# PSUM tiles per bank, reordered normalization, smaller one-hot chunks, ordered gathers and transposes with a strided output in a convolution, attention and expert kernel

## The chip, the cores and the metric

The kernel runs on one core of a Trainium2 chip. The metric is the device time of one execution in microseconds (us), taken as the median over several runs. One execution is also recorded by the hardware profiler; its span is the time from the first to the last recorded event, and its own device time lies a little above the span.

A core has several engines with queues of their own: TensorE (PE) multiplies matrices and transposes, VectorE (DVE) and ScalarE (ACT) do elementwise work, reductions and copies, GpSimd (POOL) does small vector work and issues indirect DMAs (gathers and scatters by a list of row numbers), SyncE (SP) issues most plain DMAs. SBUF is the on-chip memory of 128 partitions; PSUM is the memory that TensorE writes its results to, in banks of 512 float32 values per partition.

## The reference

The input `x` is one image of 256 channels and 48 x 48 = 2304 positions (tokens). Three layers follow one another:

1. A convolutional attention: `q`, `k` and `v` are 1x1 projections of the normalized image. They are split into 4 heads by a reshape, which makes one sequence of 9216 rows of 64 values, and `O = softmax(q k^T) v` runs over all 9216 rows. An output projection and a residual follow.
2. A "slice" attention: each token has softmax weights `sw` over 64 slices. Keys, queries and values are averaged over the tokens with these weights (`qs`, `ks`, `vs`), an attention runs among the 64 slices of each of 8 heads, and its result is spread back to the tokens with the same weights: `out = (tok spread by sw) Wout + bout`, with a residual.
3. A mixture of experts: every token is layer-normalized, a linear gate picks the best 2 of 8 experts by its logits, and each chosen expert computes `gelu(x W1 + b1) W2 + b2`. The two results, weighted by a softmax over the two logits, are added to the token.

The result goes out with channels first, as it came. Cut to its core:

```python
x = x + conv_attn(group_norm(x))      # qf, kf, vf: (9216, 64); softmax(qf kf^T / 8) vf; Wo, bo
t = tokens(x)                         # (2304, 256)
h = layer_norm(t) @ W0 + b0           # slice attention
sw = softmax(h @ Ws + bs)             # (2304, 64)
qs, ks, vs = (sum_n(sw * part) / sum_n(sw) for part in qkv(h))
tok = softmax(qs ks^T / sqrt(32)) vs  # per head, 64 x 64
t = t + (sw spread tok) @ Wout + bout
u = layer_norm(t)                     # experts
top_w, top_i = top_k(u @ Wg + bg, 2); top_w = softmax(top_w)
for e in range(8):
    t += w_dense[:, e] * (gelu(u @ W1[e] + b1[e]) @ W2[e] + b2[e])
return channels_first(t)
```

## The kernel before, in words

`layers` (L63 on) computes everything up to a token-major array `t_d` in DRAM (2304 rows of 256 values), and `to_columns` (L1238) brings it back to channels-first. The class `InOrder` (L49 to 59) wraps an engine so that its instructions keep the order in which they are written; `pe`, `dve`, `act` and `pool` are such wrappers (L78), and therefore most instructions have L57 in the profile, whatever line asked for them. What is called through `nc.` directly is placed by the scheduler of the tile framework by its own estimates. The indirect DMAs go through `pool` too, but the record of the execution shows that GpSimd did not issue the gathers in the order written.

*Start.* `x` is loaded by SP in four pieces (two for each half of the channels, 1152 positions each, L153 to 156). VectorE computes statistics over pieces of 384 positions as they come (L258 to 261), TensorE prepares the projection weights meanwhile.

*Attention.* 18 query blocks by 36 pairs of key blocks, from about 36 us to 1240 us. It is untouched.

*Slice attention* (L728 to 880). Sums over the tokens are in two banks, `bank_den` and `bank_pts`. A tile `psc` of two banks takes the scores of the 64 slices (L804); their maximum `am`, the difference `a` and an exponential follow (L815 to 821), then the values and transposes on TensorE.

*y0 stage* (L881 to 922). The 18 token tiles of 128 tokens are worked in groups of 6, 6, 4 and 2. For each tile TensorE spreads the slice result back, `swT` by `tw` (256 channels and 8 gate logits, so 264 columns), and adds the residual. The output of tile after tile goes into seven banks in turn: den, pts, the two halves of `psc`, and three more, `py0` to `py2`. VectorE takes the statistics of a tile (`bn_stats`, `bn_aggr`), ScalarE copies it to `t_sb`; for two tiles VectorE adds instead. At the end of a group VectorE adds a small constant to the variances (`ve`), GpSimd raises them to the power −1/2 (`rstd_t`) and forms `shift`, and SP stores the group to `t_d`. `normed` (L869) applies the normalization to a group on ScalarE, one instruction for each tile, into `tn2` (two buffers, so the third group waits until the first is stored) and stores it to `tn_d` in DRAM. Group 0 is normed after group 1's tiles, the others after the stage.

*Routing* (L933 to 1078). VectorE forms the logits `lg` for all tokens from the statistics, finds the best and second-best expert (`first_max`), and marks both in `both`. TensorE sums these marks over the tokens (`pto`, `pin`), and VectorE derives from the sums the position of each token and choice in a list of slots of 128 rows; 43 slots are planned, 36 of them certain to be used (`SURE`). The list itself is made by TensorE: for each of 36 (choice, token tile) pairs, a matrix `in_row` (which row of a slot, on VectorE, laid over the storage of `t_sb`) is multiplied with `what` (which slot, and the weight; the first half from VectorE and the second, in `find_tile`, from ScalarE, one instruction for each pair) and all are summed in `pw`. `find_tile` forms `in_tile` for 9, 9 and 18 pairs; the loop at L1051 works through the pairs in chunks of 3, 6, 9, 9, 6 and 3. From `pw` come the row numbers `slot_t` and the weights `slot_w`. `busy(n, spin)` issues n matmuls on TensorE whose result nobody reads.

*Experts* (L1086 to 1217). For each slot GpSimd gathers 128 normalized rows from `tn_d` by `slot_t` (`rows`), TensorE transposes them (`turn`), the two layers follow, and GpSimd adds the result `y` to `t_d` by an indirect DMA with addition. SP loads the first layer's weights of the slot's expert, 1 MB each. Rows for the slots that may be unused go into tiles of their own, `late_xs` (7 of them), and are written in the loop to come one per slot from slot 17 on.

*Back to channels first* (L1238 to 1262). Five blocks of 512 tokens (the last 256) are loaded with consecutive tokens in one partition. For each block and half of the channels, TensorE transposes four tiles into a bank `pt`, one after the other, and VectorE (first half) or ScalarE (second half) copies the bank to `ob`, writing with a stride so that the tokens come into their order. SP stores `ob`; there are three buffers of it.

Of the kernel before, what the change touches and what calls it, by code (L numbers as in the profile page):

```python
# [27 lines left out]
S = 64  # L28
# [34 lines left out]
def layers(  # L63
# [88 lines left out]
    x_sb = l0.tile([P, 2, NT], FP, name="x_sb")  # L152
    for c in range(2):  # L153
        for h in range(2):
            cols = slice(h * NT // 2, (h + 1) * NT // 2)
            nc.sync.dma_start(out=x_sb[:, c, cols], in_=x_v[:, c, cols])

# [571 lines left out]
    gating = ExitStack()  # L729
    gp = gating.enter_context(tc.tile_pool(name="gate", bufs=1))  # L730


    with tc.tile_pool(name="sa", bufs=1) as sa, sums_done, tc.tile_pool(
        name="ps_sc", bufs=1, space=PSUM
    ) as ps_sc:
        tw = sa.tile([P, C + E], FP, name="tw")
        psc = ps_sc.tile([P, 2, 512], FP, name="psc")
        banks = [bank_den, bank_pts, psc[:, 0, :], psc[:, 1, :]]

# [4 lines left out]
        with tc.tile_pool(name="ps_b", bufs=3, space=PSUM) as ps_b:  # L744
# [54 lines left out]
            for u in range(2):  # L799
                for r in range(4):  # L800
                    v, w = divmod(r, 2)
                    rows = slice(r * D1, (r + 1) * D1)
                    pe.matmul(
                        psc[w * S : (w + 1) * S, v, u * S : (u + 1) * S],  # L804
                        qk[rows, u, 0, :], qk[rows, u, 1, :], start=True, stop=True,
                    )
# [7 lines left out]

            by_head = [P, 2, 2, S]  # L815
            sc = psc[:, :, 0 : 2 * S].rearrange("p v (u t) -> p v u t", u=2)
            am = sa.tile([P, 2, 2], FP, name="am")
            dve.tensor_reduce(am, sc, AX.X, ALU.max)
            a = sa.tile(by_head, FP, name="a")
            dve.tensor_tensor(a, sc, am.unsqueeze(3).to_broadcast(by_head), ALU.subtract)  # L820
            act.activation(a, a, AF.Exp, scale=float(D1) ** -0.5)
            act.copy(vs, pv)
# [58 lines left out]
        shift = const.tile([P, NTT], FP, name="shift")  # L881
        with tc.tile_pool(name="ps_y0", bufs=1, space=PSUM) as ps_y0, tc.tile_pool(
            name="norm", bufs=2
        ) as norm:
            banks = cycle(banks + [ps_y0.tile([P, 512], FP, name=f"py{k}") for k in range(3)])
            groups = [(0, 6), (6, 6), (12, 4), (16, 2)]
            by_dve = (4, 6)
            for g, (i0, n) in enumerate(groups):
# [31 lines left out]
                )  # L920
                if g == 1:
                    normed(*groups[0])
            for group in groups[1:]:
                normed(*group)


# [6 lines left out]
    with gating, tc.tile_pool(name="onehot", bufs=1) as oh, tc.tile_pool(  # L933
# [43 lines left out]
        dve.tensor_sub(e2, m2, m1)  # L977
        act.activation(e2, e2, AF.Exp)
        act.activation(gp.tile([P, 1], FP, name="table"), e2[:, 0:1], AF.Gelu)
        upto = gp.tile([P, E, NTT], FP, name="upto")  # L980
# [69 lines left out]
        k = 0  # L1050
        for n in (3, 6, 9, 9, 6, 3):  # L1051
            ks = slice(k, k + n)
# [34 lines left out]
    with tc.tile_pool(name="ps_h", bufs=1, space=PSUM) as ps_h, tc.tile_pool(  # L1087
# [14 lines left out]
        late_xs = iter([fp.tile([P, C], FP, name=f"late_xs{s}") for s in range(SURE, NSL)])  # L1102

        def rows(s, xs):
            pool.indirect_dma_start(
                out=xs, out_offset=None, in_=tn_d[:, :],
                in_offset=bass.IndirectOffsetOnAxis(ap=slot_t[:, s : s + 1], axis=0),
                bounds_check=NT + P - 1, oob_is_err=True,
            )
            return xs  # L1110
# [36 lines left out]
        def second(s, hid, meanwhile):  # L1147
# [3 lines left out]
            for f in range(NHC):  # L1151
# [12 lines left out]
            dve.tensor_scalar(y, y, slot_w[:, s : s + 1], None, ALU.mult)  # L1164
            pool.indirect_dma_start(
                out=t_d[:, :], out_offset=bass.IndirectOffsetOnAxis(ap=slot_t[:, s : s + 1], axis=0),
# [25 lines left out]
        for s in range(SURE):  # L1192
# [17 lines left out]
            skip_runtime_bounds_check_because="it is a sum of counts, cut at NSL",  # L1210
        )
        with ExitStack() as more:  # L1212
            for s in range(SURE, NSL):
                more.enter_context(tc.If(used > s))
                if s + 1 < NSL:
                    w1[s + 1] = load_w1(s + 1)
                second(s, first(s, xT.pop(s), w1.pop(s)), lambda: turn_next(s + 1))
# [3 lines left out]
def kernel(ctx: ExitStack, tc: tile.TileContext, *args):  # L1221
# [16 lines left out]
    def to_columns():  # L1238

        sp = InOrder(tc, nc.sync)  # L1240
        with tc.tile_pool(name="fin", bufs=1) as fin, tc.tile_pool(name="fin3", bufs=3) as fin3, tc.tile_pool(
# [5 lines left out]
            for (t0, n), tt in zip(TBLOCKS, tts):  # L1247
                ob = fin3.tile([P, 2, 512], FP, name="ob", tag="ob")
                for c in range(2):
                    pt = ps_f.tile([P, 512], FP, name="pt", tag="pt")  # L1250
                    for k in range(n // P):
                        nc.tensor.transpose(  # L1252
                            pt[:, k * P : (k + 1) * P], tt[:, k, c * P : (c + 1) * P], ident
                        )

                    dst = ob[:, c, 0:n].rearrange("q (p k) -> q k p", p=P)
                    src = pt[:, 0:n].rearrange("q (k p) -> q k p", p=P)
                    if c == 0:
                        nc.vector.tensor_copy(dst, src)  # L1259
                    else:  # L1260
                        nc.scalar.copy(dst, src)  # L1261
                sp.dma_start(out=out_v[:, :, t0 : t0 + n], in_=ob[:, :, 0:n])

# [39 lines left out]
```

## Time and profile before

| what | us |
|---|---|
| median of three runs | 1619.2 (1617.68, 1619.2, 1619.96) |
| the profiled execution, device time | 1616.37 |
| its span | 1614.3 |
| TensorE busy in the span | 1569.7 |
| attention (36 to 1240) | 1204, TensorE busy 1201.98 |
| y0 stage (1263 to 1275.4) | 12.4 |
| routing (1275.4 to 1305.3) | 29.9 |
| experts (1305.3 to 1592) | 286.7, TensorE busy 283.79 |
| back to channels first (1592 to 1614.3) | 22.3, TensorE busy 6.62 |

In a row by stage, each engine has its busy time and in brackets its number of instructions; then comes the clock that TensorE was granted, as a share of full speed, the mean busy share of the 16 DMA engines, and what they moved in GB/s. A row of waits names who waited for what, the sum in us, how often, and the longest. A row in order of time has the start, the time taken, the engine, the line, the operation, what it writes and reads, how many instructions are drawn together, and in square brackets the idle time just before and what ended it.

### The profile page before, as it was taken

Reading aid. Unit: us, or ns where it says so; the run is one execution under the profiler, and the core shown is the slowest. Engines: PE = TensorE matmul, PEld = TensorE weight load, DVE = VectorE, ACT = ScalarE, POOL = GpSimd, SP = SyncE. Lnnn points to the kernel's source line nnn. Section 1 sums busy time; section 2 is a strip of 40 time slices with the busy share of each in tenths; the row PEclk is TensorE's granted clock in tenths of the full one; section 3 lists DMA queues with packets and bytes.
Section 4 is the critical chain, followed back from the end, with each engine's and each line's share of the span. In section 5 each row is a group of like instructions: output and inputs, shape, how many; then the busy total and the mean of one; then the engine's idle time right before and its main releaser. Section 6 shows DMA issues by size and latency. Waiting matters only on the chain. (4 is left out here: it accounts for less than half of the span.)

```text
span 1614.3 us, 31899 instructions
## 1 busy us (share of the span) xinstructions
PE 1569.7 (97%) x13231; PEld 786.4 (49%) x13231; DVE 1043.5 (65%) x1367; ACT 824.0 (51%) x1143; POOL 140.7 (9%) x128
## 2 busy tenths in 40 slices
PE   7999999999999999999999999999999799999995
PEld 3633343333333333333333333333334589999995
DVE  6577777777786877877868778788687721111112
ACT  2355555555655655556556555565554433333322
POOL 0000000000000000000000000000000143333321
PEclk9999999999999999999999999999999999999998
DMA  4000000000000000000000000000001856666655
GB/s 138 0 1 1 1 1 1 1 1 1 1 1 1 2 1 1 1 1 2 1 1 1 1 1 1 1 1 1 1 2 58 295 186 187 179 181 189 174 156 184
DMA packets 38246, 79.26 MB, mean 49 GB/s; under 512 B 3613, under 2 KB 23914, under 8 KB 37962
## 3 DMA queue, kind: packets, MB, share of 16 engines
q1 hardware_dynamic: 30410, 66.35, 12.3%
q0 software_dynamic: 7680, 10.75, 3.8%
q8 instruction: 108, 1.77, 0.5%
q14 instruction: 48, 0.39, 0.1%
HBM read 64.64 MB, written 12.45 MB: 48 GB/s over the span
## 5 line engine op out<-in xcount | busy, mean ns | idle before, releaser
L57 ACT ACTIVATE p<-s 128x1024 f32<-128x1024 f32 x648 | 663.5, 1024 | 489.5 <-PE s L57 479.4
L57 DVE TENSOR_TENSOR acc<-acc,p 128x1024 f32<-128x1024 f32 x612 | 748.0, 1222 | 251.8 <-ACT p L57 244.0
L57 PE MATMUL av<-p,v_sb 64*64 64x512 f32 x5184 | 676.0, 590 | 1.0 <-DVE up L57 0.7
L57 PE MATMUL s<-q,kk 64*64 64x512 f32 x5184 | 676.4, 590 | 0.0
L57 PEld LDWEIGHTS s<-q,kk 64*64 64x64 f32 x5184 | 202.2, 133 | 351.8 <-issue 181.1
L57 PEld LDWEIGHTS av<-p,v_sb 64*64 64x64 f32 x5184 | 196.1, 131 | 358.0 <-ACT p L57 202.6
L57 ACT ACTIVATE hid<-ph,bcol 128x128 f32<-128x128 f32 x312 | 89.4, 368 | 200.4 <-PE ph L57 199.7
L57 PE MATMUL py<-w_sb,hid 128*128 x624 | 147.1, 379 | 0.0
L57 PEld LDWEIGHTS ph<-xT,w 128*128 128x128 f32 x1248 | 145.3, 192 | 2.7 <-DVE xT L57 0.8
L57 PE MATMUL ph<-xT,w 128*128 128x128 f32 x1248 | 145.7, 275 | 0.5 <-DVE xT L57 0.5
L57 POOL TENSOR_TENSOR rstd_t<-ve,mhalf 128x1 f32<-128x1 f32 (+3 forms) x22 | 28.0, 1272 | 1233.4 <-DVE ve L57 1233.4
L57 DVE COPY xT<-pt 128x256 f32<-128x256 f32 x40 | 17.0, 424 | 171.6 <-PE pt L57 171.6
L57 PEld LDWEIGHTS py<-w_sb,hid 128*128 128x128 f32 x624 | 112.8, 190 | 12.2
L57 POOL DMA_INDIRECT t_d<-y,slot_t x39 | 61.7, 1583 | 98.3 <-DVE y L57 87.9
L57 DVE TENSOR_TENSOR y<-py,b_bc 128x256 f32<-128x256 f32 x39 | 16.6, 425 | 68.6 <-PE py L57 68.6
L57 POOL DMA_INDIRECT xs<-tn_d,slot_t x36 | 38.4, 1067 | 106.3 <-PE pt L57 82.1
L57 DVE RECIPROCAL rinv<-pb 128x256 f32<-128x256 f32 x18 | 31.5, 1749 | 0.0
L57 DVE TENSOR_TENSOR acc<-p 128x1024 f32<-128x1024 f32 x18 | 22.1, 1226 | 9.7 <-ACT p L57 9.7
L314 DVE TENSOR_SCALAR q<-pp,bcol 64x512 f32<-64x512 f32 (+1 forms) x30 | 20.8, 695 | 7.7 <-PE pp L297 7.4
L57 DVE TENSOR_REDUCE up<-av 128x512 f32<-128x1024 f32 x18 | 21.9, 1216 | 0.0
L319 ACT ACTIVATE kk<-pp,bcol 128x512 f32<-128x512 f32 (+1 forms) x10 | 6.4, 645 | 22.1 <-PE pp L301 22.1
L297 PE MATMUL pp<-t_sb,WqT 128*128 128x512 f32 (+1 forms) x40 | 17.6, 562 | 0.0
(281 smaller groups left out, 617.9 us busy)
## 6 DMA issues: line engine op xcount, KB each, us to landing
w<-in_L_ffn_W_dram SPq DMA_DIRECT2D x40, 1024.0 KB, 5.4
w_sb<-in_L_ffn_W_dram SPq DMA_DIRECT2D x8, 1024.0 KB, 13.1
x_sb<-in_x_dram SPq DMA_DIRECT2D x4, 576.0 KB
t<-t_d SPq DMA_DIRECT2D x4, 512.0 KB, 6.3
out_dram<-ob SPq DMA_DIRECT2D x4, 512.0 KB
t_d<-t_sb SPq DMA_DIRECT2D x2, 768.0 KB, 4.9
tn_d<-tn SPq DMA_DIRECT2D x2, 768.0 KB, 4.0
b_bc<-in_L_ffn_b_dram SPq DMA_DIRECT2D x1, 1024.0 KB
```

The lines of the kernel that those rows point to most:

```text
L57: return self.tc.keep_in_program_order(getattr(self.engine, name)(*args, **kwargs))
L297: nc.tensor.matmul(pq[:, 0:tn], WqT[:, c, cols], xn[:, c, toks], start=(c == 0), stop=(c == 1))
L314: nc.vector.tensor_scalar(dst, pq[rows, 0:tn], bcol[rows, B_Q + m : B_Q + m + 1], 0.125, ALU.add, ALU.mult,)
L319: nc.scalar.activation(kk[:, m, toks], pk[:, 0:tn], AF.Identity, bias=bk_m)
```

## The change

- The second half of `x` by channels is loaded in pieces of 1152, 768 and 384 positions; there are five loads in place of four.
- `psc` becomes two tiles of one bank each. The maximum, the difference and the exponential of the scores are made for each bank.
- `normed` of groups 0 and 1 comes after the whole y0 stage, followed by 13 `busy` matmuls. `normed` of groups 2 and 3 comes in the routing, after the exponential `e2` and ahead of the activation that loads the table for Gelu. The pool `norm` therefore lives longer; it still has two buffers.
- The chunks are 3, 6, 6, 3, 6, 6, 3, 3.
- Every indirect DMA is given an order behind the one written before it (`indirect`). On GpSimd the seven gathers of `late_xs` now come one in each of the slots 17 to 23; before, they came among the first gathers.
- In `to_columns` the transposes write with a stride, so that the bank holds the tokens in their order, and the copies to `ob` read and write contiguously. ScalarE's copies keep their written order, and the last two blocks are stored by ScalarE's queue in place of SP's.

```diff
-    for c in range(2):
-        for h in range(2):
-            cols = slice(h * NT // 2, (h + 1) * NT // 2)
-            nc.sync.dma_start(out=x_sb[:, c, cols], in_=x_v[:, c, cols])
+    for c, pieces in enumerate(((1152, 1152), (1152, 768, 384))):
+        at = 0
+        for n in pieces:
+            nc.sync.dma_start(out=x_sb[:, c, at : at + n], in_=x_v[:, c, at : at + n])
+            at += n
...
+    norm = gating.enter_context(tc.tile_pool(name="norm", bufs=2))
...
-        psc = ps_sc.tile([P, 2, 512], FP, name="psc")
-        banks = [bank_den, bank_pts, psc[:, 0, :], psc[:, 1, :]]
+        psc = [ps_sc.tile([P, 512], FP, name=f"psc{v}") for v in range(2)]
+        banks = [bank_den, bank_pts, *psc]
...
-            dve.tensor_reduce(am, sc, AX.X, ALU.max)
-            a = sa.tile(by_head, FP, name="a")
-            dve.tensor_tensor(a, sc, am.unsqueeze(3).to_broadcast(by_head), ALU.subtract)
-            act.activation(a, a, AF.Exp, scale=float(D1) ** -0.5)
+            a = sa.tile([P, 2, 2, S], FP, name="a")
+            for v in range(2):
+                dve.tensor_reduce(am[:, v, :], sc[v], AX.X, ALU.max)
+            for v in range(2):
+                dve.tensor_tensor(a[:, v], sc[v], bc(am[:, v, :], [P, 2, S]), ALU.subtract)
+                act.activation(a[:, v], a[:, v], AF.Exp, scale=float(D1) ** -0.5)
...
-                if g == 1:
-                    normed(*groups[0])
-            for group in groups[1:]:
+            for group in groups[:2]:
                 normed(*group)
+            busy(13, spin)
...
         act.activation(e2, e2, AF.Exp)
+        for group in groups[2:]:
+            normed(*group)
         act.activation(gp.tile([P, 1], FP, name="table"), e2[:, 0:1], AF.Gelu)
...
-        for n in (3, 6, 9, 9, 6, 3):
+        for n in (3, 6, 6, 3, 6, 6, 3, 3):
...
+        issued = []
+        def indirect(**kwargs):
+            new = nc.gpsimd.indirect_dma_start(**kwargs)
+            if issued:
+                tc.add_manual_dep(
+                    new.ins, issued[-1].ins.name,
+                    mybir.DependencyInfo(mybir.DependencyClass.NoSync, mybir.DependencyReason.DATA),
+                    reason="in written order",
+                )
+            issued.append(new)
...
-            pool.indirect_dma_start(
+            indirect(
                 out=xs, out_offset=None, in_=tn_d[:, :],
...
-        sp = InOrder(tc, nc.sync)
+        sp, act = InOrder(tc, nc.sync), InOrder(tc, nc.scalar)
...
+                    by_row = pt[:, 0:n].rearrange("q (p k) -> q k p", p=P)
                     for k in range(n // P):
-                        nc.tensor.transpose(
-                            pt[:, k * P : (k + 1) * P], tt[:, k, c * P : (c + 1) * P], ident
-                        )
-                    dst = ob[:, c, 0:n].rearrange("q (p k) -> q k p", p=P)
-                    src = pt[:, 0:n].rearrange("q (k p) -> q k p", p=P)
+                        nc.tensor.transpose(by_row[:, k, :], tt[:, k, c * P : (c + 1) * P], ident)
                     if c == 0:
-                        nc.vector.tensor_copy(dst, src)
+                        nc.vector.tensor_copy(ob[:, c, 0:n], pt[:, 0:n])
                     else:
-                        nc.scalar.copy(dst, src)
-                sp.dma_start(out=out_v[:, :, t0 : t0 + n], in_=ob[:, :, 0:n])
+                        act.copy(ob[:, c, 0:n], pt[:, 0:n])
+                queue = act if t0 >= TBLOCKS[-2][0] else sp
+                queue.dma_start(out=out_v[:, :, t0 : t0 + n], in_=ob[:, :, 0:n])
```

More of the change, by code (lines that the diff above doesn't have):

```diff
@@ L803, in layers @@
                     pe.matmul(
-                        psc[w * S : (w + 1) * S, v, u * S : (u + 1) * S],
+                        psc[v][w * S : (w + 1) * S, u * S : (u + 1) * S],
                         qk[rows, u, 0, :], qk[rows, u, 1, :], start=True, stop=True,
@@ L813, in layers @@
             pe.matmul(pv, dr[0:1, :], bvrow, start=False, stop=True)
-            by_head = [P, 2, 2, S]
-            sc = psc[:, :, 0 : 2 * S].rearrange("p v (u t) -> p v u t", u=2)
+            sc = [psc[v][:, 0 : 2 * S].rearrange("p (u t) -> p u t", u=2) for v in range(2)]
             am = sa.tile([P, 2, 2], FP, name="am")
-            dve.tensor_reduce(am, sc, AX.X, ALU.max)
-            a = sa.tile(by_head, FP, name="a")
-            dve.tensor_tensor(a, sc, am.unsqueeze(3).to_broadcast(by_head), ALU.subtract)
-            act.activation(a, a, AF.Exp, scale=float(D1) ** -0.5)
+            a = sa.tile([P, 2, 2, S], FP, name="a")
[4 more added lines that the diff above has]
+                act.activation(a[:, v], a[:, v], AF.Exp, scale=float(D1) ** -0.5)
             act.copy(vs, pv)
@@ L881, in layers @@
         shift = const.tile([P, NTT], FP, name="shift")
-        with tc.tile_pool(name="ps_y0", bufs=1, space=PSUM) as ps_y0, tc.tile_pool(
-            name="norm", bufs=2
-        ) as norm:
+        with tc.tile_pool(name="ps_y0", bufs=1, space=PSUM) as ps_y0:
             banks = cycle(banks + [ps_y0.tile([P, 512], FP, name=f"py{k}") for k in range(3)])
@@ L1164, in second @@
             dve.tensor_scalar(y, y, slot_w[:, s : s + 1], None, ALU.mult)
[L1165 removed]
+            indirect(
                 out=t_d[:, :], out_offset=bass.IndirectOffsetOnAxis(ap=slot_t[:, s : s + 1], axis=0),
@@ L1211, in layers @@
         )
+        issued.clear()
         with ExitStack() as more:
             for s in range(SURE, NSL):
+                issued.clear()
                 more.enter_context(tc.If(used > s))
```

## The prediction

> **What bounds the kernel now.** I read the table by stage first, then TensorE's waits in the stretch that the change touches, then the order of time there.
>
> ```profile
> core 0: us, PE busy (x) PEld busy (x) DVE busy (x) ACT busy (x) POOL busy (x), PEclk, DMA share, GB/s
> 36.00:1240.00 1204.00, 1201.98 (x10859) 462.85 (x10857) 923.64 (x1037) 691.13 (x727) 22.35 (x16) 1.00 0.01 1
> 1263.00:1275.40 12.40, 12.31 (x60) 6.97 (x60) 9.76 (x38) 6.90 (x17) 4.21 (x7) 1.00 1.05 363
> 1275.40:1288.40 13.00, 5.01 (x18) 4.37 (x18) 10.23 (x37) 9.19 (x21) 2.22 (x6) 0.74 0.73 248
> 1305.30:1592.00 286.70, 283.79 (x1953) 264.83 (x1953) 48.10 (x124) 89.40 (x312) 103.49 (x80) 1.00 0.64 177
> 1592.00:1614.30 22.30, 6.62 (x36) 6.17 (x36) 4.73 (x5) 4.73 (x5) 1.15 (x1) 0.70 0.65 223
> ```
>
> TensorE fills 1204 us of attention and 287 us of experts to over 98%; the change does not touch those instructions. What it can win lies in the routing (1275 to 1305) and the last 22 us, where TensorE is idle or slowed, and in a few waits:
>
> ```profile
> PE pto L57 <- DVE e L57: 8.1, 1, 8.1
> PE pt L57 <- DMA xs<-tn_d,slot_t: 1.8, 2, 1.0
> PE pw L57 <- ACT what L57: 1.4, 2, 0.9
> ```
>
> The 8.1 us is VectorE's routing chain. It starts at the last tile of the y0 stage and ends at `slot_t` (1300.88), behind which all gathers stand.
>
> **The routing, step by step.** ScalarE's order of time shows why the chain starts late:
>
> ```profile
> 1275.14 0.63 ACT L57 COPY t_sb<-py 128x264 f32<-128x264 f32 x2
> ...
> 1277.11 0.38 ACT L57 COPY t_sb<-psc 128x264 f32<-128x264 f32 x1 [0.50 <-DVE s L57]
> 1277.38 5.02 ACT L57 ACTIVATE tn<-t_sb,shift,rstd_t 128x256 f32<-128x256 f32 x10
> 1284.28 1.09 ACT L57 ACTIVATE tn<-t_sb,shift,rstd_t 128x256 f32<-128x256 f32 x2 [1.88 <-DMA tn_d<-tn]
> ...
> 1294.11 4.09 ACT L57 ACTIVATE what<-in_tile,wk 128x43 f32<-128x43 f32 x18 [0.64 <-DVE in_tile L57]
> ```
>
> 1. *Start of the chain.* Six `normed` activations (about 0.50 us each) stand ahead of the last `t_sb` copies, which therefore run to 1277.5. The two tiles in `psc` share one tile: the statistics of the second wait for the copy of the first (0.23 us twice in the middle of the stage, 0.63 at its end, 1276.64). With a tile per bank and the copies first, only TensorE's last y0 matmul limits (end 1275.3): last statistics 1275.35 to 1275.96, `ve` at 1276.1, GpSimd's power 0.73 from 1276.36, so `lg<-lg,rstd_t` at 1277.1 instead of 1278.41: **−1.3**.
>
> 2. *Thirteen filler matmuls.* The clock here:
>
> ```profile
> 1280.00:1283.00 3.00, 0.00 (x0) 0.00 (x0) 2.69 (x10) 2.40 (x5) 0.00 (x0) 0.50 0.81 277
> ```
>
> A filler at full clock takes 0.43 us (18 instructions, 4.09 us); 13 take 5.6, from 1275.3 to 1280.9. `both`, which `pto` waits for, comes at about 1281.7, so nothing queues behind them. The pair `pto`, `pin` (0.82 and 0.69 at half clock) is read in by VectorE some **0.3** earlier. `in_tile` then starts at 1286.15 instead of 1287.81. If they came too late they would cost their overhang, at most some 0.5.
>
> 3. *`normed` of the last two groups behind the exponential.* ScalarE: copies to 1276.1; twelve `normed` to 1282.15; exponential. The third group needs the first one's store landed (two buffers). Those stores now stand behind the `t_d` stores on SP: issue near 1279.2, plus 3.8 to 4.0 (the median of `tn_d` stores), so 1283.1. Four `normed` (2.0) to 1285.1; the fourth group waits for the second store, issued 1282.25, to 1286.05, and ends at 1287.15; table load 1.28 and one activation 0.20: `what` starts at **1288.7**, although `in_tile` is ready at 1286.7. So the wait for the store moves to ScalarE's routing work: 2 us of lateness. What is late next: SP issues the last `tn_d` store at 1287.2, ahead of the weight loads (1291.71 before) and 8 us ahead of the first gather that must see it landed. TensorE reads 36 `what` at 0.234 us each (the last 18 in 4.22), ScalarE makes them at 0.2275 (18 in 4.09), so by this path the `pw` matmuls end about 9.05 after the first `what`, at 1297.75.
>
> 4. *Chunks of six.* VectorE's path: after `in_tile` (first nine) 3.0 us to the second `in_tile` before; with 6 and 3 in place of 9 two more pairs of small instructions, about 0.15 each beyond the elements. The last `in_tile` comes at 1291.6, its first six one-hot rows at 1293.9 (0.42 and 0.95 after its 0.96), where before nine were waited for. TensorE then needs 18 times 0.234 = 4.2: end 1298.2 against 1300.31. That is later than ScalarE's 1297.75, so it sets the end: **−2.1** for steps 1 to 4 together, of which the chunks are some 0.4. The ScalarE wait has only 0.45 us of cover left: a store that lands 1 us later takes 0.5 away, 3 us later takes all.
>
> **Gathers.** GpSimd issues in an order that put seven late ones ahead:
>
> ```profile
> 1303.70 1.01 POOL L57 DMA_INDIRECT xs<-tn_d,slot_t  x1 [0.30 <-issue]
> 1305.02 1.01 POOL L57 DMA_INDIRECT late_xs<-tn_d,slot_t  x1 [0.30 <-issue]
> ...
> 1311.62 1.01 POOL L57 DMA_INDIRECT xs<-tn_d,slot_t  x1 [0.30 <-issue]
> ```
>
> The third `xs` comes behind five `late_xs` at 1311.62; TensorE waits 0.81 us for it (1315.94). Chained, it issues 1.32 after the second, and the wait goes: **−0.8**. The late gathers now go one each into slots 17 to 23. GpSimd there has 1.59 for a `t_d` store, 1.07 for the gather, 1.3 with gap for the late one: about 4 of 7.24 us per slot, cover enough; cost 0, and without that cover 1.3 at most per slot on a `y` ring of two, which still hides it.
>
> **The tail.** The copies write with a stride:
>
> ```profile
> 1600.73 1.07 DVE L1259 COPY ob<-pt 128x512 f32<-128x512 f32 x1 [9.42 <-PE pt L1252]
> 1603.97 1.09 DVE L1259 COPY ob<-pt 128x512 f32<-128x512 f32 x1 [0.63 <-PE pt L1252]
> 1605.68 1.06 DVE L1259 COPY ob<-pt 128x512 f32<-128x512 f32 x1 [0.62 <-ACT ob L1261]
> ```
>
> and ScalarE's last in the chain of waits is `1603.12 1.09 ACT`, then 2.8 us of an output store. A contiguous copy of the same size takes 0.586 on ScalarE (the L244 copies) and about 0.69 on VectorE (`q<-pp`, 512 elements, 0.695). So stores leave 0.4 to 0.5 earlier. But the DMA engines are full through most of 1597 to 1610 except 0.63 near 1603 and 0.70 near 1605; stores sooner fill part of those: −0.3 to −0.9, I take **−0.5**. Two stores on ScalarE's queue save at most SP's 0.37 per issue, which is not what they wait for (they wait for landed buffers, ring of three): 0. On ScalarE the issue of block 3 now stands ahead of block 4's copy and waits for VectorE's half; that block waits for store 1 to land anyway (1607.03): 0, at worst 0.4.
>
> The other side of it is that 36 transposes now write with a stride of up to 16 bytes in PSUM. No row shows that. [...] The nearest row is the strided copy: 1.07 us per 512, 2.1 ns an element, 0.27 for 128. The transposes already take 0.229 each at half clock (16 in 3.66), so that price is nearly covered there and only the warm ones (about 0.12) would stretch: 36 x 0.27 = 9.7 against 6.71 now, so the last store goes 2.0 to 3.0 later, and the end moves about +1.2, since the DMA backlog is gone by then (R2 has the sum). [...] by the row's other reading (the write keeps up with the stream of columns) −0.5. I take −0.5: a transpose streams at 1.8 ns a column, near the strided element.
>
> [...] Row: 0.37 per issue. If that were on the path it would be −0.4; with full DMA engines I take 0.
>
> **Rest.** `x_sb` in 768 and 384: VectorE's statistics run on to 11.4 without idle behind the loads, and TensorE waits for a weight matrix at 10.38 and is busy to 12.3: 0 (−0.1 to +0.2, a fifth issue). Two `am`, `a`, exponentials in place of one: about 0.2 of overhead at 1256.4 to 1257.9, behind TensorE's `pv` and token sums (to 1258.4): 0, at worst +0.2.
>
> **Sum.** −2.1 −0.8 −0.5 = −3.4. The profiled execution took 1616.37 (span 1614.3 and 2.07 around it), so it becomes 1613.0. The median of the runs is 2.8 above this execution; less 3.4 it is **1615.8**.
>
> **Rivals.**
> - *R1, the moved `normed` eats the routing gain* (0.26). DMA is saturated until 1278 and the two `tn_d` stores now go behind 2.3 MB of `t_d`; if they land 2 us later, `what` starts at 1290.7, the matmuls end at 1299.75, gain 0.6, and with gathers and tail −1.9: 1617.3. For it: ScalarE already waits 1.88 for such a store. Against it: traffic is thinner after 1280 (share 0.81).
> - *R2, slower: strided PSUM writes slow the transposes.* Place: L1252's 36 transposes. Price: behind the last transpose come a copy (0.4), an issue (0.4), the landing of 256 KB [...], and 3.9 us from the end of the DMA traffic (1610.4) to the end of the span. The end is then 1605.8 + 36 x, against 1614.3. It cancels the other gains of 2.9 from x = 0.32 us, and is measurably slower from 0.41. At 0.54 (twice the strided copy's price): tail +10.9, total +8.0: 1627.2. [...] Chance 0.06.
> - *R3, more is won* (0.18): ScalarE's stores land in 3 us, the tail closes both DMA gaps (−0.9), the chunks let TensorE follow VectorE without idle (another −0.5), the start saves 0.1: −4.6, 1614.6.
> - *R4, the change does nothing*: the gather order or the banks do not set the time. The 0.81 wait and the 0.63 are in the trace, so this is only part of R1.
>
> **How the numbers follow.** The measurement tells ±0.2% (3.2 us): faster is below 1616.0. Likeliest case 0.50: 1614.8 to 1617.0, of it 0.40 under the limit and 0.10 above; R3 0.18 faster; R1 0.26 (with it the transposes at 0.27 us, total −1.7), of it 0.02 faster; R2 0.06, 0.05 of it slower. Faster 0.60, same 0.35, slower 0.05. The range 1613.2 to 1618.2 holds the first case, most of R1 and of R3, and leaves out R2.
>
> **What would show it.** Right: no idle of VectorE for `t_sb` in the stage; `lg*rstd` 1.3 earlier; PEclk 1.00 from 1276 to 1281; `slot_t` 2.1 earlier; no wait for `xs` at the third slot; copies of 0.6 to 0.7 and transposes as before. Wrong: ScalarE waits over 3 us for `tn_d` and TensorE's `pw` for `what`; transposes over 0.3 us; statistics waiting for x.

## The result and the profile after

The changed kernel takes 1613.25 us (median of 7, 1611.19 to 1613.73) against 1618.99 (median of 7, 1616.96 to 1619.96) for the kernel before: ratio 0.9965, 95% interval 0.9954 to 0.9977. That is 5.7 us less. The forecast was 1615.8, or 3.4 us less. The time lies at the low edge of the range (1613.2 to 1618.2) and the direction is right, but the gain is 1.7 times the forecast.

The two profiled executions differ by less than the medians: 1616.37 before, 1612.46 after, spans 1614.3 and 1610.5. This table cuts both spans at four marks: the start of the first statistics of the y0 stage, the start of the instruction that writes `slot_t`, the issue of the last `t_d` store, and the end.

| stretch | before | after | difference | forecast |
|---|---|---|---|---|
| start to first y0 statistics | 1263.75 | 1263.44 | −0.31 | 0 |
| y0 stage and routing, to `slot_t` | 37.13 | 35.45 | −1.68 | −2.1 |
| experts, to the last `t_d` store | 290.71 | 289.72 | −0.99 | −0.8 |
| tail, to the end | 22.74 | 21.86 | −0.88 | −0.5 |

Between these two executions the forecast's sum nearly holds (−3.9 against −3.4). The other 1.8 us of the medians' difference is not in this pair; the experiments look for it.

TensorE's waits of the changed kernel, from 1260 us to 1595 us:

```profile
PE pex L57 <- DVE used_i L57: 2.0, 1, 2.0
PE pto L57 <- ACT tn L57: 1.3, 1, 1.3
PE pt L57 <- DMA xs<-tn_d,slot_t: 1.0, 1, 1.0
PE pw L57 <- ACT what L57: 0.6, 1, 0.6
PE ph L57 <- DVE xT L57: 0.5, 1, 0.5
```

The wait of 8.1 us for the routing chain is now filled by 5.78 us of fillers and 1.3 of idle. The second wait for `xs` (0.81 us, in the third slot) is gone. The wait ahead of `pex` has grown from 0.8 us to 2.0.

Its ScalarE, in order of time:

```profile
1275.76 6.00 ACT L57 ACTIVATE tn<-t_sb,shift,rstd_t 128x256 f32<-128x256 f32 x12
1281.70 0.22 ACT L57 ACTIVATE e<-e 128x18 f32<-128x18 f32 x1
1282.61 2.07 ACT L57 ACTIVATE tn<-t_sb,shift,rstd_t 128x256 f32<-128x256 f32 x4 [0.69 <-DMA tn_d<-tn]
1285.54 1.09 ACT L57 ACTIVATE tn<-t_sb,shift,rstd_t 128x256 f32<-128x256 f32 x2 [0.86 <-DMA tn_d<-tn]
...
1288.06 8.29 ACT L57 ACTIVATE what<-in_tile,wk 128x43 f32<-128x43 f32 x36
```

The two waits for stores are there as forecast (0.69 and 0.86 us), and `what` starts at 1288.06 where 1288.7 was expected. The 36 `what` now run without a gap.

The stretch of the `pw` matmuls in the changed kernel, by the microsecond (columns as in the table by stage):

```profile
1286.00:1287.00 1.00, 0.00 (x0) 0.00 (x0) 0.97 (x3) 0.98 (x3) 0.00 (x0) 1.00 1.01 348
...
1289.00:1290.00 1.00, 1.00 (x7) 1.00 (x7) 0.97 (x3) 1.00 (x6) 0.00 (x0) 0.50 0.03 8
1290.00:1291.00 1.00, 1.00 (x6) 1.00 (x6) 1.00 (x3) 1.00 (x6) 0.00 (x0) 0.50 0.46 37
...
1292.00:1293.00 1.00, 1.00 (x11) 1.00 (x11) 0.96 (x3) 0.88 (x5) 0.00 (x0) 1.00 0.96 397
```

TensorE stands idle around 1286 with its clock still granted in full. It pays a little later: the clock is 0.50 from 1288.6 to 1292.0 (one stretch of 3.41 us), and six or seven matmuls are at work in a microsecond there in place of eleven. In the kernel before, the half-clock stretch (1280 to 1287) lay ahead of `pw`.

GpSimd's gathers and the first copies of the tail, changed kernel:

```profile
1300.09 1.33 POOL L1110 DMA_INDIRECT xs<-tn_d,slot_t  x1 [22.53 <-DVE slot_w L57]
1301.72 1.01 POOL L1110 DMA_INDIRECT xs<-tn_d,slot_t  x1 [0.30 <-issue]
1303.99 1.01 POOL L1110 DMA_INDIRECT xs<-tn_d,slot_t  x1 [1.26 <-PE pt L57]
```

```profile
1597.71 0.69 DVE L1272 COPY ob<-pt 128x512 f32<-128x512 f32 x1 [9.38 <-PE pt L1270]
1599.26 0.69 DVE L1272 COPY ob<-pt 128x512 f32<-128x512 f32 x1 [0.86 <-PE pt L1270]
...
1602.93 0.69 DVE L1272 COPY ob<-pt 128x512 f32<-128x512 f32 x1 [2.04 <-DMA out_dram<-ob]
```

The third gather goes out 3.9 us after the first (9.6 before), as soon as its buffer is free. The copies take 0.69 us in place of 1.07, but the fourth waits 2.04 us for a store to land. What that wait costs, the last experiment tells.

### The profile page after: what moved, and what is told of

Same layout as the page of the kernel before. It is cut to its first block, busy times and chain, and to the rows that moved or that the text cites. A ratio compares the mean times of both kernels' runs of the same rounds, so it can differ in the third digit from the quotient of the medians.

```text
span 1610.5 us, 31964 instructions
## 1 busy us (share of the span) xinstructions
PE 1573.3 (98%) x13257; PEld 790.1 (49%) x13257; DVE 1041.9 (65%) x1373; ACT 822.2 (51%) x1144; POOL 141.1 (9%) x128
## 4 chain that ended last, share of the span: by engine, by line
PE 94%; DMA 2%; DVE 1%; ACT 1%; issue 1%; SPq 0%; POOL 0%; POOLq 0%; ACTq 0%; DVEq 0%
PE s L57 34%; PE av L57 34%; PE ph L57 8%; PE py L57 8%; PE pa L57 1%; PE pb L57 1%; PE pp L298 1%; PE pw L57 1%; DMA t_d<-y,slot_t 1%; PE pp L327 1%; PE pp L302 1%; PE pt L57 1%; ACT tn L57 0%; DMA Wq_raw<-in_L_conv_Wq_dram 0%; ACT p L57 0%
```

## The experiments

The working theory is that the stage gains add up as in the table. Its first rival is that something else, not in this pair of profiles, makes the kernel before slower in most executions. Each median below is compared with the kernel before on the same chip. In each profile I read the same marks.

### A second profile of the kernel before

No edit.

> The kernel before, unedited, for a second profile. The two profiles on hand differ by 3.8 us of span, but the medians by 5.7. Theory A (chance in single executions): TensorE was granted half its clock for 3.4 us near 68 us in the first profile of before, and one matmul group near 15 us took 1.2 us longer in the profile of the changed kernel; both are accidents, so a second profile of before shows neither at the same place or with the same size, its span lies near 1616 to 1617.5, and its stages from 1240 us on have the same lengths as in the first (routing from the first y0 statistics to slot_t 37.1 us, last t_d store to the end of the span 22.7) within 0.2. Theory B (something systematic in the first 70 us differs by the edit of the x loads): the second profile shows Wq landing at 10.4 and the first projection group taking 2.35 as in the first one, and the half-clock stretch again.

It took 1620.9 us (12 executions) beside 1619.5 in 15 other executions of the same kernel on that chip (ratio 1.0004, 0.9995 to 1.0013). The profiled execution took 1619.1, 2.7 us more than the first profile. Its stretches: 37.15 for y0 stage and routing and 22.84 for the tail, as in the first profile; but 293.98 for the experts in place of 290.71. TensorE's waits from 1299 to 1330 us, then the table from 1312:

```profile
PE ph L57 <- DVE xT L57: 3.1, 2, 2.6
PE pt L57 <- DMA xs<-tn_d,slot_t: 1.0, 1, 1.0
```

```profile
1312.00:1314.00 2.00, 0.47 (x2) 0.47 (x3) 0.42 (x1) 0.99 (x4) 1.43 (x2) 0.78 0.22 72
1314.00:1316.00 2.00, 2.00 (x11) 2.00 (x11) 0.00 (x0) 0.15 (x1) 1.60 (x2) 0.50 0.88 234
1316.00:1318.00 2.00, 2.00 (x18) 2.00 (x17) 0.00 (x0) 0.50 (x2) 0.00 (x0) 0.87 1.03 422
```

TensorE was idle for 2.6 us in slot 1, and about 3.4 us at half clock followed (an estimate from the granted clock of the three rows: 0.78, 0.50 and 0.87), in which one set of 32 matmuls took 5.25 us in place of 3.73. Together that is 4.1 of the 4.3 us by which the expert stretch is longer than in the changed kernel (289.72).

Theory A fell: the span is 1617.1 at the edge of what it allowed, because the expert stretch was 3.3 us longer and not within 0.2. But Wq was read at 9.89 us with the old loads, where B wanted 10.4, so B's first part fell as well. Whether TensorE had half its clock near 68 us again was not shown. What makes the kernel before slow is at the start of the experts.

### The chain of gathers alone, and alone undone

The kernel before with only the chain:

```diff
-            pool.indirect_dma_start(
+            indirect(
                 out=xs, out_offset=None, in_=tn_d[:, :],
```

> The kernel before with the chain of indirect DMAs alone. In the first profile of before the unchained gathers cost TensorE 0.81 us (slot 2 waits for its rows); in the second one VectorE, ScalarE and SP stood still together until 1313.0, TensorE waited 2.6 us for xT in slot 1, a half-clock window of 3.4 us followed, and slot_t to the last t_d store took 293.98 us in place of 290.71. Theory A (the seven early late_xs gathers cause both): this stretch takes 289.7 as in the changed kernel, the single times scatter less than before's (1617.8 to 1622.7 in 15 executions) and the median gains 1 to 4 us, about 2.5. Rival B (the pause is chance and hits any order): only the 0.8 to 1.0 us of the first profile is won, and the scatter stays 4 to 5 us wide.

The changed kernel with only the chain undone:

```diff
-            if issued:
+            if False:
                 tc.add_manual_dep(
```

> The changed kernel with the chain alone undone, so seven late gathers go ahead of the third again. Theory A (the chain is the largest single part by the medians): slot_t to the last t_d store takes 290.7 to 294 us in place of 289.7, the median lies 1 to 4 us above the changed kernel's, and the single times scatter over 3 us or more. Rival B (the order of gathers is worth 0.8 to 1.0 and no more): median 0.8 to 1.0 above, scatter like that of the changed kernel (1611.2 to 1613.7).

Both ran on one chip, where the kernel before took 1615.93 us (60 executions, 1614.01 to 1616.90). The chain alone took 1614.98 (ratio 0.9994, 0.9985 to 1.0002), so 0.95 less, which the interval does not tell from nothing; its expert stretch is 289.67. On that chip rival B's size was right; before scattered over 2.9 us there, the chain alone over 2.8. Without the chain the changed kernel took 1614.96 (0.9993, 0.9987 to 1.0000), some 2 us more than two other variants of it on the same chip (1612.98 and 1613.08, below). Its profile happened to be of its slowest execution (1617.39 us) and shows the loss:

```profile
1309.24 3.73 PE L57 MATMUL ph<-xT,w 128*128 128x128 f32 x32
1315.16 0.44 PE L57 MATMUL pt<-ident,xs 128*128 128x128 f32 x2 [2.19 <-DMA xs<-tn_d,slot_t]
1315.44 4.01 PE L57 MATMUL py<-w_sb,hid 128*128 x10
```

The third slot's rows are 2.19 us late, and behind the idle time the clock falls to 0.50 from 1315.6 to 1319.0: `py` x10 takes 4.01 us in place of 2.32. Idle and slow clock make 3.9; the expert stretch is 293.75, 4.0 more than with the chain. Theory A held here in all its points: the stretch, the median, and a scatter of 4.1 us (1613.33 to 1617.39). The parts do not simply add: on this chip the chain is worth 0.95 alone and some 2 in the changed kernel.

The chain puts the additions to `t_d` in order too, not only the gathers. In the traces of these two runs, of the kernel before and of the changed one, the sequence of GpSimd's 82 indirect DMAs differs only in the places of the seven late gathers, and in that the fifth gather without the chain goes out ahead of the first addition. So it is the gathers that count.

To see whether this also explains the other chips, the chain alone was run again.

> The kernel before with the chain of indirect DMAs alone, a second time. On the chip of its first run before took 1615.9 and the chain won 0.95; on another chip before took 1619.5 to 1620.9, while all kernels with the chain took 1612.4 to 1613.3 on both. Theory A (what differs between chips and executions is how long the gathers out of order, and the half-clock window behind them, hold TensorE): where before takes over 1618 again, the chain alone takes 1614.5 to 1615.5 and wins 3 to 5 us; where before takes under 1617, it wins about 1. Rival B (another part of the change removes the difference between chips): the chain alone moves with before, and wins about 1 on either.

This time the kernel before took 1621.01 us on its chip (9 executions, 1617.55 to 1622.63), and the chain alone 1615.15 (6 executions, 1614.68 to 1615.89): ratio 0.9966, 0.9954 to 0.9979, so 5.9 us, at the top of theory A's 3 to 5 and above it. Its time hardly depends on the chip (1614.98 and 1615.15), while that of before goes from 1615.9 to 1621.0. In this profile and the first one of the chain alone TensorE's waits at the start of the experts are those of the changed kernel:

```profile
PE pt L57 <- DMA xs<-tn_d,slot_t: 1.0, 1, 1.0
PE ph L57 <- DVE xT L57: 0.5, 1, 0.5
```

In all eleven profiles with the chain the expert stretch is 289.64 to 289.76; in the three without it 290.71, 293.75 and 293.98. So the chain is worth 1 to 6 us, by chip and execution. What the slow executions of before on this last chip lose, no profile shows; none was taken of it there. The rest of the change adds 2.0 to 2.3 to it: 1615.15 against 1612.86 without the first fillers, which were found to be worth nothing, and 1614.98 against 1612.98 with the old chunks, likewise. On the chip of the first measurement that leaves 5.7 − 2.1, about 3.6 us, for the chain, an estimate by subtraction.

### The filler that was missing

```diff
-        busy(7, spin)
+        busy(12, spin)
```

> The changed kernel with 12 filler matmuls in place of 7 behind pin. In the changed kernel TensorE is idle from 1285.4 to 1287.6 and again 0.6 before pw, and the granted clock is 0.50 from 1288.2 to 1291.7, in the first third of the pw matmuls. Theory A (this clock gap costs): no half-clock stretch in the pw matmuls; their end moves from 1298.3 to about 1297.7 (then VectorE's one-hot rows set the end: pair 18's ready at 1293.55, and 18 times 0.234), so slot_t and the span about 0.5 earlier. Rival B (ScalarE's what sets the end, and the clock cost is hidden behind it): the end of pw stays within 0.15 of 1298.3. Rival C (the fillers delay pex and with it expert_i on VectorE): slot_t later by 0.3.

It took 1612.41 us (0.9952, 0.9935 to 0.9968). y0 stage and routing: 35.05 us, 0.40 less than in the changed kernel. (Four profiles have the changed kernel's routing as it is, its own and those of the variants in gathers, loads and copies: 35.28 to 35.45, mean 35.37.) TensorE's clock in the same place:

```profile
1286.00:1288.00 2.00, 1.70 (x9) 1.09 (x7) 1.93 (x8) 1.97 (x5) 0.00 (x0) 1.00 0.78 271
1288.00:1290.00 2.00, 1.70 (x15) 1.70 (x16) 1.97 (x5) 2.00 (x11) 0.00 (x0) 1.00 0.11 37
```

Theory A holds, at 0.3 to 0.4 in place of 0.5. The half-clock stretch costs that much, which is the whole shortfall of the routing: 37.13 − 35.05 = 2.08, and 2.1 was forecast.

### Three buffers of normed tiles

```diff
-    norm = gating.enter_context(tc.tile_pool(name="norm", bufs=2))
+    norm = gating.enter_context(tc.tile_pool(name="norm", bufs=3))
```

> The changed kernel with three buffers of normed tiles in place of two, so that the third and fourth group wait for no store of tn_d (the third has a buffer of its own, the fourth one that was stored by 1282.6). Theory A (ScalarE's wait for the stores, 0.69 and 0.86 us, costs nothing to the end because TensorE and VectorE set it): what starts near 1286.5 in place of 1288.06, and slot_t moves by less than 0.2 unless the clock changes with it. Rival B (the prediction's thin cover of 0.45 us was in truth none, ScalarE sets the end): slot_t 1 us or more earlier. Rival C: pw starts earlier, near 1287.9, TensorE's idle stretch is shorter and no half-clock window falls in pw: slot_t about 0.5 earlier by the clock and not by the wait; then the granted clock between 1286 and 1292 is 1.00.

1612.63 us (0.9954, 0.9937 to 0.9970). `what` starts 0.59 us after `in_tile` in place of 2.23, and the stretch is 35.06, the same as with the longer filler. The granted clock is 1.00 from 1286 to 1294. TensorE's matmuls here:

```profile
1288.20 0.27 PE L57 MATMUL pex<-ident,ex 128*1 128x128 f32 x1 [2.03 <-DVE used_i L57]
1288.31 0.80 PE L57 MATMUL pw<-what,t_sb 128*128 128x128 f32 x6
```

The numbers are rival C's: 0.4 by way of the clock, none by the wait itself, since the kernel with the longer filler still has the wait and is as fast. But C's reason holds only in part. The idle time of 0.59 us ahead of `pw` is gone, that of 2.0 us ahead of `pex` is as long as in the changed kernel. That the clock stayed full is known of this one execution; how often it would was not shown.

### The fillers behind the y0 stage taken out

```diff
-            busy(13, spin)
```

> The changed kernel without the 13 filler matmuls behind the y0 stage. The prediction gave them 0.3 us (pto and pin at full clock) and no cost. Theory A: TensorE is idle from 1274.7 to 1281.7, the clock falls to half near 1279 for 6.8 us, pto and pin take 0.82 and 0.69, scan starts 0.3 later; but the half-clock window then lies ahead of the pw matmuls and not in their first third, so pw loses nothing there and slot_t comes at the same time as in the changed kernel or up to 0.3 earlier. Rival B (the window falls into pw all the same): slot_t 0.3 to 0.5 later.

1612.86 us on the third chip, stretch 35.37 against 35.45, inside the scatter given above. The scan (VectorE's first reading of `pto`) starts 0.34 later after the first statistics (19.21 against 18.87), but the slow clock lies from 1278 to 1285 and `pw` runs at full clock. Theory A holds: the 13 fillers save 0.34 and move the slow stretch into `pw`, which costs it again. They need the longer second filler to be worth anything.

### Chunks as before

```diff
-        for n in (3, 6, 6, 3, 6, 6, 3, 3):
+        for n in (3, 6, 9, 9, 6, 3):
```

> The changed kernel with chunks of 3, 6, 9, 9, 6, 3. The prediction gave the smaller chunks 0.4 us. Theory A (VectorE's one-hot rows set the end of pw): pair 18's rows come 0.5 us later and the end of pw with them, slot_t 0.3 to 0.6 later than 1298.9, if the granted clock in pw is the same. Rival B (TensorE, slowed to half clock in the first third and continuous from there to the end, sets it): slot_t within 0.1.

1612.98 us, stretch 35.46 against 35.45: rival B. While TensorE runs the 72 `pw` records back to back behind a slow start (9.90 us in both kernels), earlier rows are of no use. Whether the chunks gain anything at full clock was not tried.

### Normed groups as before

```diff
                     in_=t_sb[:, these, 0:C],
                 )
+                if g == 1:
+                    normed(*groups[0])
-            for group in groups[:2]:
+            for group in groups[1:]:
                 normed(*group)
             busy(13, spin)
...
-        for group in groups[2:]:
-            normed(*group)
```

> The changed kernel with the normed groups where they were (group 0 after group 1's tiles, the others behind the stage and ahead of the exponential); the banks as tiles of their own are kept. Theory A (the two edits share the gain of 1.3 us from the stage's first statistics to lg times rstd, 14.66 before and 13.37 after: the banks take the waits of VectorE away, the order takes the last t_sb copies forward): last statistics as in the changed kernel (11.6 after the first), lg times rstd 0.5 to 0.8 later than there (13.9 to 14.2), and what starts near 1288.4, as both have a wait for the tn_d stores. Rival B (the banks do it all): 13.4. Rival C (the order does it all): 14.6.

1613.46 us, stretch 35.81. From the first statistics to `lg` times `rstd` it takes 13.37 us, exactly as in the changed kernel: rival B, the banks do the whole 1.3. What the order of the normed groups changes comes later, in VectorE:

```profile
1284.33 0.17 DVE L57 TENSOR_SCALAR w1st<-e 128x18 f32<-128x18 f32 x1 [0.69 <-ACT e L57]
```

The exponential stands behind a normed group that waits 1.95 us for its store, VectorE waits 0.69 for it, and `slot_t` comes 0.36 later. In the kernel before VectorE was itself so late that this wait lay hidden; with the banks split it comes out, and the move of the groups takes it away.

### The loads of x as before

```diff
-    for c, pieces in enumerate(((1152, 1152), (1152, 768, 384))):
+    for c in range(2):
+        for h in range(2):
```

> The changed kernel with x loaded in four pieces as before. The prediction gave the five loads 0 (-0.1 to +0.2). In the profile of the changed kernel Wq landed 0.42 us earlier (9.96 in place of 10.38). Theory A (the loads did it): Wq lands at 10.3 to 10.5 again, the first projection starts 0.4 later (15.99), and the median is about 0.4 above the changed kernel's. Rival B (chance in the arrival): Wq lands between 9.8 and 10.2 still, and the median doesn't move.

1612.57 us (0.9955, 0.9939 to 0.9972), Wq read at 10.12 us, a first projection group of 3.00 us. Rival B: in all profiles TensorE first reads Wq between 9.85 and 10.45 us with either form of the loads. The −0.31 in the table's first row is such a difference. For the half-clock stretch near 68 us (in the first profile of before the mean granted clock from 68 to 72 us is 0.57, in the changed kernel's 1.00) it was not shown whether the loads have a part in it.

### Strided copies as before

```diff
-                        nc.tensor.transpose(by_row[:, k, :], tt[:, k, c * P : (c + 1) * P], ident)
+                        nc.tensor.transpose(
+                            pt[:, k * P : (k + 1) * P], tt[:, k, c * P : (c + 1) * P], ident
+                        )
...
-                        nc.vector.tensor_copy(ob[:, c, 0:n], pt[:, 0:n])
+                        nc.vector.tensor_copy(dst, src)
```

> The changed kernel with contiguous transposes and strided copies, the two last stores still by ScalarE. In the changed kernel the 36 strided transposes took 5.76 us from the first to the last and 16 of them at half clock 3.30, against 6.71 and 3.66 before, so no price of the stride is seen. Theory A (the copies' stride is what cost): copies of 1.07 us again, the first store 0.5 us later, and from the last t_d store to the end of the span 22.3 to 22.7 us in place of 21.9. Rival B (the tail is bound by the DMA engines and the copies don't matter; what was won came from the queue): 21.8 to 22.0.

1613.08 us. The copies take 1.07 us again, and the tail is 22.76 us, just above theory A's range and far from rival B's. But the changed kernel's own 21.86 is the shortest of eight tails with contiguous copies and three buffers (up to 22.85, mean 22.48); the five with strided ones lie from 22.74 to 23.22 (mean 22.88). From the first transpose to the end the means are 14.55 and 15.10. So the contiguous copies are worth 0.4 to 0.55 us and not the 0.88 of the table. Four of the five strided tails also store by SP alone; the one of this run, which doesn't, is 0.28 above the mean, or 0.53 from the first transpose on. By medians this kernel can't be told from its neighbours.

### A version with four further edits

12 fillers behind `pin`, three buffers of normed tiles, the last `in_tile` in two halves, five buffers `ob`:

```diff
-            elif k == 18:
-                find_tile(18, 18)
+            elif k in (18, 27):
+                find_tile(k, 9)
```

> The changed kernel with four further edits: 12 fillers behind pin in place of 7, three buffers of normed tiles, in_tile of the last 18 pairs in two halves of 9 (chunks 3, 6, 6, 3, 6, 3, 6, 3), and five buffers ob in the last stage. Theory: from the first y0 statistics to slot_t 35.05 with the fillers alone; the halved in_tile (0.55 in place of 0.96) brings pair 18's rows 0.4 forward: 34.65, against 35.45 in the changed kernel; the tail from the start of the transposes to the end 14.1 to 14.3 in place of 14.5, since no copy waits for a store to land. Sum -1.0 to -1.2 us against the changed kernel, so a median near 1612. Rival: ScalarE's what, one by one at 0.2275, now sets the end of pw, and only 0.4 is won; and the tail is bound by the DMA engines, 0.

1612.60 us (0.9948, 0.9931 to 0.9965), beside 1612.86 and 1613.46 of its neighbours on that chip. The stretch is 35.10 and not 34.65: the second half of `in_tile` now stands between the rows of the last 18 pairs, ScalarE's `what` wait for it (0.37 us twice) and TensorE for them (0.26 to 0.37 us three times), so VectorE's sum of work is the bound. From the first transpose to the end it takes 14.54, the mean of the others: with five buffers for five blocks no copy has a store to wait for, and the buffers `ob` bring nothing. The rival's sizes held, though not its reason for `pw`. It is no better, as far as can be measured, than the longer filler alone.

## Why the prediction was right or wrong

*Start of the chain, −1.3:* right. From the first statistics to `lg` times `rstd` it went from 14.66 to 13.37. The step named two causes, the shared tile and the copies behind `normed`; only the first was at work.

*Thirteen fillers, −0.3:* right for the scan (0.34 by the experiment), wrong in the sum. The step asked what queues behind the fillers. It did not ask what a clock kept at full speed leads to: the 14 filler records behind `pin` end in 3.19 us in place of 4.28, TensorE runs dry for 2.0 us, and the slow stretch comes in `pw`.

*`normed` behind the exponential:* right that ScalarE's lateness stays covered. The stores landed sooner (1282.6 where 1283.1 was assumed). R1 did not happen.

*Chunks of six, some 0.4 of the −2.1:* not borne out. The end of `pw` was forecast at 1298.2 from VectorE's rows and came at 1298.3, but TensorE's clock set it. With the clock restored the whole stretch is 2.08 shorter, so the forecast's sum for the routing was right at full clock.

*Gathers, −0.8:* the term that was mis-sized. The mechanism is the one named (the third gather behind late ones), and in the first pair of profiles it is worth 0.99. But the 0.81 us wait that it was priced from is the smallest in three profiles of this order. In the two others TensorE waited 2.19 us for its rows and 2.6 us for `xT`, and about 3.4 us at a granted clock of 0.50 followed. Measured: 0.95 us on one chip, 5.9 on another. The profiled execution lay 2.8 us under the median of its kernel, and the forecast carried that over as an offset: 1613.0 for the profiled execution became 1615.8 for the median. The changed kernel's median of 1613.25 is near the first of these. As the later runs suggest, much of the offset was what the change removes.

*The sum, −3.4:* in part luck. Between the two profiles it is nearly right, term by term. By medians what the change wins goes by the chip, since the time of before does and that of the changed kernel hardly: some 3 us on the chip where before took 1615.9, some 8 where it took 1621.0, both read from variants whose edits were worth nothing. R3 (1614.6) asked for more than the sum, by stores that land sooner, a fuller tail and the chunks; not these made the difference, but the gathers.

*Tail, −0.5:* right; 0.4 to 0.55 by the means. R2 did not happen. In both kernels the transposes (128 float32 columns each, in the changed one with a stride of up to four elements) start 0.21 us apart at half clock and 0.11 us apart at full clock, so no price of the stride is seen in them. That ScalarE's queue is worth nothing was not tried by itself.

*x loads, 0:* right. The pair of `am` and `a` on two banks: from the score matmuls (1255.58 and 1255.26) to the first y0 statistics it is 8.17 and 8.18 us, so nothing.

## What to carry to other kernels

Here the fillers that kept TensorE's clock at 1.00 also made what followed end earlier (14 filler records in 3.19 us in place of 4.28), and the slow stretch landed on the work: behind 2.02 and 0.59 us of idle time the `pw` matmuls had a clock of 0.50 for 3.41 us. Follow the row of the clock to the next gap, and try what a filler there does; here it was worth 0.3 to 0.4 us. A wait read in one profile is one draw; where transfers are issued in an order nobody wrote down, look at the scatter of the times and at how far the profiled execution lies from the median before pricing the order by that wait. And means over several profiles of the same stretch tell a half microsecond that medians of the whole time can't.

## What had not been expected of the hardware

The kernel before took 1615.9, 1619.0, 1619.5 to 1620.9 and 1621.0 us in four series of runs, three of them known to be on different chips, while variants with the gathers in order agreed within 1.1 us (1612.4 to 1613.5, or 1615.0 and 1615.2 for the chain alone). In the second profile of the kernel before, VectorE and ScalarE both went on at 1313.0. First the two rows of the first profile, then the same two of the second:

```profile
1310.08 1.14 ACT L57 ACTIVATE hid<-ph,bcol 128x128 f32<-128x128 f32 x4 [0.64 <-PE ph L57]
1310.30 0.42 DVE L57 COPY xT<-pt 128x256 f32<-128x256 f32 x1 [4.15 <-PE pt L57]
```

```profile
1313.01 1.14 ACT L57 ACTIVATE hid<-ph,bcol 128x128 f32<-128x128 f32 x4 [4.21 <-remote]
1313.05 0.42 DVE L57 COPY xT<-pt 128x256 f32<-128x256 f32 x1 [7.54 <-remote]
```

(`remote` stands where the profile found no instruction that ended the wait.) Both waits are 3.4 to 3.6 us longer than in the first profile. In the second profile the records of the TensorE matmuls that write `ph` and `pt` end at 1309.41 and 1309.62 (such ends are modelled), and ScalarE and VectorE go on 3.60 and 3.43 us after them; in the first profile it is 0.04 us for both. GpSimd issued gathers in that time, at 1309.63, 1310.95 and 1312.26. The delay is in none of the profiles with the chain. On which side it lies, what it is, and whether the late gathers lead to it, stays open.

The slow stretches of the first profile of before and of the changed kernel's profile, beside the idle time of TensorE that each of them began in or came behind:

| profile | TensorE idle, us | granted clock 0.50, us |
|---|---|---|
| before | none (busy from 64 to 72) | 68.11 to 71.53 |
| before | 1275.32 to 1283.39 | 1279.85 to 1286.67 |
| before | 1590.46 to 1599.43 | 1593.87 to 1604.11 |
| before | 1606.14 to the end | 1610.94 to the end |
| changed | 1285.54 to 1287.57 and 1287.84 to 1288.43 | 1288.59 to 1292.00 |
| changed | 1587.48 to 1596.43 | 1592.38 to 1599.20 |
| changed | 1602.18 to the end | 1606.03 to the end |

Elsewhere from 60 us on these two profiles have a clock of 1.00, also around an idle stretch of 1.28 us (changed kernel, 1280.51 to 1281.79) and one of 1.02 us (before, 1304.23 to 1305.25).

The same gap ahead of `pw` did not always end in a slow stretch. With 2.03 us idle ahead of `pex` and 0.44 us within `pw` (three buffers) the clock was 1.00 from 1286 to 1294, and with 0.60 us ahead of `pw` alone (longer filler) likewise. With 2.79 us ahead of `pex` (normed groups as before) it was 0.50 from 1288 to 1290. What decides was not shown, and with one profile of each variant the numbers do not say how often it happens.
